# Moving the helper work of a fused attention and feed-forward kernel to other places of the step: constants, norm transposes and first weights

## The chip, the cores and the metric

The kernel runs on one core of a Trainium2 chip. The metric is the device time of one execution in microseconds (us); lower is better. A core has five engines that run their own instruction queues in order: PE (TensorE, matrix products), DVE (VectorE), ACT (ScalarE), POOL (GpSimd) and SP (SyncE, which here issues the DMAs). The PE writes into PSUM, which this kernel uses as six banks of 128 x 512 fp32 for products (tag "mm") and one double bank for attention scores (tag "st").

## The reference, cut to what matters

Two layers, each an attention over a context followed by a feed-forward, on 2048 tokens of width 512 (32 sequences of 64).

```python
x = x + L0_xattn(layernorm(x), ctx)      # 32 query heads, 8 key/value heads, rotary, softmax
x = x + L0_ffn(layernorm(x))             # gate and up weights 4-bit, group scales and zeros
x = x + L1_xattn(layernorm(x), ctx)      # like L0, with norms of q and k in place of the rotary
x = x + L1_ffn(layernorm(x))             # a small memory with a gate

# L0_ffn: w = sc[g] * (nibble(qw) - (nibble(qz[g]) + 1)), 512 x 2752 and 1376 x 512
w_gu = dequant(qweight_gu, qzeros_gu, scales_gu, g_idx_gu)
gate, up = (x @ w_gu)[..., :1376], (x @ w_gu)[..., 1376:]
out = (silu(gate) * up) @ dequant(qweight_down, qzeros_down, scales_down, g_idx_down)
```

The change touches the first attention (L0_xattn) and the way from it into L0_ffn.

## The kernel before, in words

**Tiling.** The 2048 tokens are four chunks of 512 (`NCH = 4`, index c). Attention goes over 8 key/value heads (index g, four query heads each) and, inside, over the four chunks: 32 **steps** (g, c), the loop in `Attention.run`. Large products are done as seven smaller ones instead of eight (a Strassen scheme, `PRODUCTS`, `quarters`), which needs sums of blocks first: `left_sums` and `right_sums`, four POOL instructions of 128 x 512 each.

**One step on the PE.** The loop is software-pipelined. In the pass for step i the PE does, in this order: the rest of the output products of step i-1 (`O`, 40 matmuls, `output_rest`), the key projection of step i+1 (`pk`), the query projection of step i+1 (`P`, 56 matmuls, `project_q`), the values' products of step i (`po`, 32), the value projection of step i+1 (`pv`, 32), the first output products of step i (`O`, 16, `output_first`), and the scores of step i+1 (`S`, 32). I count a step's length from one start of `pk` to the next.

**Beside it.** DVE does the softmax of step i while `output_rest` runs (`softmax`, a generator: mask on S L531, row maximum r2x and m1x, its spread mb L313, subtraction L581, sum r2s and m1s, reciprocal L586, spread ib L313), mixed with the additions of the output products to x (`join` L242). ACT does the exponential; POOL multiplies by the reciprocal sums (s L589). Then come the rotations (`rotate`): for k (rk) and for each of four quarters of q (rq), two ACT copies, a cosine product L424, a sine product L425 on DVE, and a sum on POOL L426 (kT, qT). The temporary tile of `rotate` (`tmp_tile`) has two buffers, shared with the constants below. POOL also makes the sums of the attention output (oT, `left_sums`, L166 to L169) in each step, in the steps with c = 0 the sums of the output weights (wo, `right_sums`, L174 to L177), and in the steps with c = 3 those of the next query weights (wq).

**Order.** Each engine's order is made ahead of time by a list scheduler: of the instructions that it takes to be ready, the one written first goes first; one that is not ready is passed over. `tc.issue_after(ins)` queues what a block emits on the engine of `ins` behind `ins`, without a wait, and leaves other engines alone.

**The pieces.** `ffn_constants` is a generator of 24 pieces that build the dequantisation tables of L0_ffn (scales split in three bf16 parts, zeros, one-hot group rows; tiles pidx, scales_gu, scales_down, qz, zi, g_idx_*, szoh). Through `late` one piece runs in each step of g = 1 to 6: one that prepares pidx (20 tiny instructions), seven of scales (three DMAs, then CAST, SCALAR_TENSOR_TENSOR, CAST, SCALAR_TENSOR_TENSOR, CAST), eight of zeros (shift, cast, shift, cast), eight of indices (one DMA, four instructions). All but the DMAs is DVE work. Before the change a piece is emitted just behind `output_rest`, and queued behind the last join (`self.added`).

**The way into the feed-forward.** When a chunk's last output is joined (g = 7, one step later), `joined` takes its norm statistics, and `after` scales it (xnb, DVE L272), transposes it on the PE (xtb, 16 matmuls L286), copies it (ACT L290, xnT) and makes its sums (POOL). In the pass for (7, c) this is done for chunk c-1. Before the change `after` is emitted ahead of `values` for c = 1 and 2, behind it for c = 3.

`ahead` has three hooks for the pass (7, 2), which bring in the first feed-forward weights wgu: `ffn_load` (8 DMAs), `ffn_dequant` for each quarter k of the rows (nibbles by a DVE shift L900, two matmuls pgz L917 that spread scales and zeros, two DVE instructions L895 and L896), and `ffn_sums` (POOL). Hook 0 stands behind `project_q`, hook 1 behind `values`, hook 2 ahead of `output_first`. In the last pass (7, 3), `tail` starts the feed-forward's first up product (`P<-xnT,wgu`).

Of the kernel before, what the change touches and what calls it, by code (L numbers as in the profile page):

```python
# [15 lines left out]
ALU = mybir.AluOpType  # L16
# [28 lines left out]
def tile_xattn_ffn_2_layers(ctx: ExitStack, tc: tile.TileContext, a: dict, out: bass.AP):  # L45
    nc = tc.nc
# [30 lines left out]
    def w_tile(name):  # L77
        return wp.tile([P, NBLK, 2, HC], F32, tag="w", name=name, bufs=2)
# [7 lines left out]
    def tmp_tile(name):  # L86
        return ap_.tile([P, 2, CH], F32, tag="tmp", name=name)
# [26 lines left out]
    sinT = const.tile([P, KH, 4, KB], F32, tag="sinT", name="sinT")  # L114
# [48 lines left out]
    def left_sums(t, width=HC, engine=nc.gpsimd):  # L163
        b = [t[:, k, :, 0:width] for k in range(NBLK)]
        tt = engine.tensor_tensor
        tt(b[4], b[2], b[3], ALU.add)  # L166
        tt(b[5], b[4], b[0], ALU.subtract)
        tt(b[2], b[0], b[2], ALU.subtract)
        return tt(b[6], b[1], b[5], ALU.subtract).ins  # L169
# [152 lines left out]
    class Attention:  # L322
# [94 lines left out]
        def rotate(self, name, src, dst, view, over):  # L417

            t = tmp_tile(name)
            h = HD // 2  # L420
            for lo, hi in ((0, h), (h, HD)):
                nc.scalar.copy(t[lo:hi, 1], src[HD - hi : HD - lo])  # L422
            x = t[:, 0] if src.space == bass.MemoryType.PSUM else src
            nc.vector.tensor_tensor(view(x), view(src), over(cosT), ALU.mult)  # L424
            nc.vector.tensor_tensor(view(t[:, 1]), view(t[:, 1]), over(sinT), ALU.mult)  # L425
            nc.gpsimd.tensor_tensor(dst(None), dst(x), dst(t[:, 1]), ALU.add)  # L426

        def project_q(self, g, c):
# [243 lines left out]
        def run(self, hooks, joined, after, between=lambda c: None, tail=lambda: None, late={},  # L672
                ahead=(lambda: None,) * 3):

            steps = [(g, c) for g in range(NKV) for c in range(NCH)]  # L680

            def ctx_of(i):
                return load_ctx(steps[i][1], f"{self.L}_{steps[i][0]}_{steps[i][1]}")

            before = None
            v = self.v
            ctxT = ctx_of(1)
            (kT, kpart), (qT, part) = self.state
            scales = self.norms(0, 0, kpart, part)
            st = self.scores(0, 0, kT, qT)  # L690
            for i, (g, c) in enumerate(steps):
                more = i + 1 < len(steps)
                if c == NCH - 1 and g + 1 < NKV:
                    self.load_kv(g + 1)
                for hook in hooks.get((g, c), ()):
                    hook()
                ctx_next = ctx_of(i + 2) if i + 2 < len(steps) else None
                if g == NKV - 1 and c > 1:
                    between(c - 2)
                pieces = self.softmax(g, c, st, scales)  # L700

                def middle():
                    if c == NCH - 1 and g + 1 < NKV:
                        with tc.issue_after(self.pooled):
                            left_sums(self.wq[g + 1])

                if before is not None:
                    probs = self.output_rest(*before, pieces, middle)
                    with tc.issue_after(self.added):
                        for hook in late.get((g, c), ()):  # L710
                            hook()
                else:
                    *_, probs = pieces
                if c == 0 and g > 0:
                    self.load_out(g)
                done = before is not None and before[0] == NKV - 1
                if done:
                    joined(before[1])
                if more:
                    kT, kpart = self.project_k(*steps[i + 1], ctxT)  # L720
                    if c == 0:
                        right_sums(self.wo[g])
                    qT, part = self.project_q(*steps[i + 1])
                    if c == NCH - 2 and g + 1 < NKV:
                        self.load_q(g + 1)
                    if i + 2 == len(steps):
                        ahead[0]()
                else:
                    tail()

                late_after = not more and self.L == 0
                if done and not late_after:
                    after(before[1])
                oT = self.values(g, c, v, probs)
                if done and late_after:
                    after(before[1])
                if i + 2 == len(steps):
                    ahead[1]()
                if more:
                    scales = []  # L740

                    def middle():
                        scales.append(self.norms(*steps[i + 1], kpart, part))

                    v = self.project_v(*steps[i + 1], ctxT, middle)
                    scales = scales[0]
                if self.L == 1 and more:
                    with tc.issue_after(self.pooled):
                        self.pooled = left_sums(oT)
                else:  # L750
                    self.pooled = left_sums(oT)
                if i + 2 == len(steps):
                    with tc.issue_after(self.pooled):
                        ahead[2]()
                before = self.output_first(g, c, oT)
                if more:
                    with tc.issue_after(last_matmul):
                        st = self.scores(*steps[i + 1], kT, qT)
                ctxT = ctx_next
            between(NCH - 2)  # L760
            self.output_rest(*before)
            joined(before[1])
# [97 lines left out]
    def ffn_load(i):  # L860
        f0, fw = groups[i]
        w = w_tile(f"wgu{i}")
        for k in range(KT):
            for j in range(2):
                nc.sync.dma_start(
                    w[:, 2 * j + k // 2, k % 2, 0:fw].bitcast(U32),
                    a["qweight_gu"][16 * k : 16 * k + 16, j * INTER + f0 : j * INTER + f0 + fw]
                    .unsqueeze(1)
                    .to_broadcast([16, 8, fw]),
                )  # L870
        wgu[i] = w
# [32 lines left out]
    def ffn_dequant(i, *parts):  # L904

        f0, fw = groups[i]
        sz, oh = ffn["sz"], ffn["oh"]
        w, d = wgu[i], wd[i] if i in wd else None
        for k in parts:
            if k < KT:  # L910
                wk = w[:, k // 2 : 4 : 2, k % 2, 0:fw]
                nibbles(wk, P)
                pp = [mm_tile(f"pgz{i}_{k}_{side}") for side in range(2)]
                for side, rows in enumerate(
                    (slice(R_GS, R_GS + 3 * NG), slice(R_GZ, R_GZ + NG))
                ):
                    nc.tensor.matmul(  # L917
                        pp[side][:, 0 : 2 * fw],
                        oh[rows, k * P : (k + 1) * P],
                        sz[rows, :].rearrange("p (j f) -> p j f", j=2)[:, :, f0 : f0 + fw],  # L920
                        start=True,
                        stop=True,
                    )
                pv = [x[:, 0 : 2 * fw].rearrange("p (j f) -> p j f", j=2) for x in pp]
                dequant(wk, pv[0], pv[1])
                continue
            if k - KT >= len(ffn_tiles(i)):
                continue
            t = k - KT
            f, w_ = ffn_tiles(i)[t]  # L930
            dt = d[0:w_, 2 * t : 2 * t + 2, 0, :]
            nibbles(dt, w_)
            pp = [mm_tile(f"pdz{i}_{t}_{side}") for side in range(2)]
            for side, rows in enumerate((slice(R_DS, R_DS + 3 * NGD), slice(R_DZ, R_DZ + NGD))):
                nc.tensor.matmul(
                    pp[side][0:w_, :], oh[rows, f : f + w_], sz[rows, 0:D], start=True, stop=True
                )
            dequant(dt, *(x[0:w_, :].rearrange("p (j w) -> p j w", j=2) for x in pp))

    def ffn_sums(i):  # L940
        left_sums(wgu[i], groups[i][1])
# [391 lines left out]
    def first_after(c):  # L1333
        norm_apply(c, "b")
        if c == last - 1:
# [7 lines left out]
        tail=ffn_first,  # L1343
        late={(g, c): [lambda: next(pieces, None)] for g in range(1, NKV - 1) for c in range(NCH)},
        ahead=(
            lambda: (ffn_load(0), ffn_dequant(0, 0, 1)),
            lambda: ffn_dequant(0, 2, 3),
            lambda: ffn_sums(0),
        ),
    )  # L1350

# [126 lines left out]
```

## Time and profile before

| | us |
|---|---|
| median of 3 runs | 2862.06 (2861.47 to 2863.86) |
| the profiled execution's own time | 2860.84 |
| its span, first to last instruction | 2859.1 |
| PE busy | 2804.8 (98%) |
| DVE busy | 1874.9 (66%) |
| POOL busy | 1318.9 (46%) |
| ACT busy | 834.0 (29%) |

Times in the timeline are us from the span's start. The first attention lies at about 15 to 1190 us, its feed-forward up to about 1600 us, the second attention after it. A busy share is an average; a PE that is 98% busy still has places where it waits, or where it counts as busy and runs slowly. The profile also gives the TensorE clock that was granted: over the whole span 0.995 of full speed.

### The profile page before, as it was taken

The numbers are of one execution on the slowest core, as the hardware profiler recorded it, in microseconds if no ns is written. First come the engines' busy times: TensorE is split into PE (matmuls) and PEld (weight loads), VectorE is DVE, ScalarE is ACT, GpSimd is POOL, SyncE is SP. The second block draws the span as 40 slices with busy tenths as digits, with TensorE's granted clock in tenths as the row PEclk, the third lists the DMA queues.
The fourth block names the chain that finished last, engine by engine and source line by source line (L and its number), as shares of the span: only waits on it lengthen the run. The fifth ranks groups of instructions, "written<-read, shape, count | busy, mean of one in ns | idle before, by whom it ended". The sixth has DMA issues, their size and how long they took to land. (4 is left out here: it accounts for less than half of the span.)

```text
span 2859.1 us, 41235 instructions
## 1 busy us (share of the span) xinstructions
PE 2804.8 (98%) x16742; PEld 2267.1 (79%) x16742; DVE 1874.9 (66%) x2814; ACT 834.0 (29%) x1410; POOL 1318.9 (46%) x1030
## 2 busy tenths in 40 slices
PE   7999999999999999999999999999999999999997
PEld 5878787888888887888888778888888888888775
DVE  7777777777777777665555655555555555555666
ACT  3333333333333333221111222222222222222333
POOL 5554545454545454544433444444444444444331
PEclk9999999999999999999999999999999999999999
DMA  4111111111111110100001101111111111111101
GB/s 159 38 52 46 53 46 53 44 53 45 53 47 52 50 55 15 45 23 22 16 13 33 52 30 59 45 52 45 52 45 52 45 52 45 52 45 52 30 1 59
DMA packets 103812, 130.77 MB, mean 46 GB/s; under 512 B 8725, under 2 KB 65165, under 8 KB 103623
## 3 DMA queue, kind: packets, MB, share of 16 engines
q1 hardware_dynamic: 103047, 127.09, 13.7%
q8 instruction: 133, 2.18, 0.3%
q10 hardware_dynamic: 576, 1.05, 0.1%
q14 instruction: 56, 0.46, 0.1%
HBM read 123.92 MB, written 4.19 MB: 45 GB/s over the span
## 5 line engine op out<-in xcount | busy, mean ns | idle before, releaser
L189 PE MATMUL O<-wo,oT 128*128 128x256 f32 x3584 | 802.4, 381 | 1.8 <-ACT oT L617 1.1
L189 PE MATMUL P<-xnT,wq 128*128 128x256 f32 x3584 | 788.2, 380 | 10.6 <-ACT h L214 10.4
L189 PEld LDWEIGHTS P<-xnT,wq 128*128 128x128 f32 x3584 | 681.1, 190 | 133.4 <-issue 31.5
L189 PEld LDWEIGHTS O<-wo,oT 128*128 128x128 f32 x3584 | 670.2, 190 | 115.5 <-issue 25.0
L242 DVE TENSOR_TENSOR x<-x,O 128x512 f32<-128x512 f32 (+1 forms) x448 | 368.4, 823 | 248.2 <-PE O L189 248.1
L589 POOL TENSOR_TENSOR s<-s,ib 128x512 f32<-128x512 f32 x128 | 169.4, 1344 | 529.9 <-DVE ib L313 514.0
L214 ACT COPY h<-P 128x512 f32<-128x512 f32 (+1 forms) x352 | 202.7, 576 | 561.2 <-PE P L189 559.4
L247 POOL TENSOR_TENSOR qr<-qs,nhalf 128x20 f32<-128x20 f32 x32 | 113.4, 3544 | 380.5 <-DVE qs L496 380.5
L426 POOL TENSOR_TENSOR qT<-h,rq 128x512 f32<-128x512 f32 x128 | 175.5, 1371 | 237.5 <-DVE rq L425 237.5
L583 ACT ACTIVATE s<-s 128x1024 f32<-128x1024 f32 x64 | 67.7, 1057 | 728.2 <-DVE s L581 728.2
L189 PE MATMUL P<-xnT,wgu 128*128 128x256 f32 (+1 forms) x1232 | 271.3, 380 | 0.2
L189 PEld LDWEIGHTS P<-xnT,wgu 128*128 128x128 f32 (+1 forms) x1232 | 229.8, 187 | 39.9 <-DVE x L242 4.1
L407 PE MATMUL pv<-wkv,ctxT 128*128 128x128 f32 x1984 | 248.2, 281 | 1.2 <-DVE h L439 1.2
L407 PEld LDWEIGHTS pv<-wkv,ctxT 128*128 128x128 f32 x1984 | 230.5, 193 | 23.1 <-issue 17.6
L375 PE MATMUL pk<-ctxT,wkv 128*128 128x512 f32 x496 | 223.2, 592 | 0.9 <-DVE h L439 0.9
L422 ACT COPY rq<-h 64x512 f32<-64x512 f32 x256 | 157.9, 617 | 123.6 <-DVE h L439 115.6
L424 DVE TENSOR_TENSOR h<-h,cosT 128x512 f32<-128x512 f32 x128 | 91.6, 716 | 123.0 <-ACT rq L422 122.8
L375 PEld LDWEIGHTS pk<-ctxT,wkv 128*128 128x128 f32 x496 | 94.1, 190 | 94.0 <-issue 89.6
L457 DVE TENSOR_TENSOR qT<-h,P 128x512 f32<-128x512 f32 x128 | 87.7, 686 | 100.8 <-PE P L189 94.7
L463 DVE TRANSPOSE_TENSOR_REDUCE part<-q 128x16 f32<-128x512 f32 x128 | 90.6, 708 | 87.8 <-ACT q L459 83.9
L960 DVE TENSOR_TENSOR h<-h,P 128x512 f32<-128x512 f32 (+1 forms) x96 | 61.2, 640 | 127.1 <-PE P L189 94.2
L967 POOL TENSOR_TENSOR hT<-h,h 128x512 f32<-128x512 f32 (+1 forms) x48 | 56.6, 1183 | 186.9 <-DVE h L960 186.9
(250 smaller groups left out, 3429.9 us busy)
## 6 DMA issues: line engine op xcount, KB each, us to landing
ctxT<-in_ctxT SPq DMA_DIRECT2D x62, 1024.0 KB
wq<-in_L_wq SPq DMA_DIRECT2D x32, 256.0 KB
wo<-in_L_wo SPq DMA_DIRECT2D x32, 256.0 KB
wq<-in_L_wqT SPq DMA_DIRECT2D x32, 256.0 KB
wo<-in_L_woT SPq DMA_DIRECT2D x32, 256.0 KB
wgu<-in_qweight_gu SPq DMA_DIRECT2D x40, 128.0 KB
out<-o SPq DMA_DIRECT2D x16, 256.0 KB
x<-in_x SPq DMA_DIRECT2D x12, 256.0 KB
```

Of the source, the lines that this page charges most:

```text
L189: ins = nc.tensor.matmul(pv[0:w, m, :], left[:, l, k, m * P : m * P + w], right[:, r, k, :], start=(first and m == 0 and k == 0), stop=(k ...
L214: last_copy = nc.scalar.copy(t[size], ps[size]).ins
L242: return nc.vector.tensor_tensor(dst, dst, src, ALU.add).ins
L247: return nc.gpsimd.tensor_tensor(dst, src, nhalf[:, : src.shape[-1]], ALU.pow).ins
L375: nc.tensor.matmul(ps, wkv[:, k, 0, :], ctxT[:, k, :], start=(k == 0), stop=(k == KT - 1))
L407: nc.tensor.matmul(ps[:, t * HD : (t + 1) * HD], ctxT[:, k, t * P : (t + 1) * P], wkv[:, k, 1, :], start=(k == 0), stop=(k == KT - 1),)
L422: nc.scalar.copy(t[lo:hi, 1], src[HD - hi : HD - lo])
L424: nc.vector.tensor_tensor(view(x), view(src), over(cosT), ALU.mult)
L426: nc.gpsimd.tensor_tensor(dst(None), dst(x), dst(t[:, 1]), ALU.add)
L457: nc.vector.tensor_tensor(q, xv, yv, ALU.add)
L463: nc.vector.tensor_reduce(part[:, i, f], q2.rearrange("p (g q) -> p g q", q=KB), AX.X, ALU.add, apply_transpose=True,)
L589: nc.gpsimd.tensor_tensor(sv[:, f], sv[:, f], ib[:, f * W : (f + 1) * W].unsqueeze(1).to_broadcast([P, KH, W]), ALU.mult,)
```

## The change

Three things are moved; no arithmetic is changed.

1. A piece of `ffn_constants` is emitted behind `project_v` of the pass in place of behind `output_rest`, and its DVE work is queued behind `self.turned`, the last sine product of the next queries' rotation.
2. In L0, for the passes (7, 1) and (7, 2), `after` (norm scaling, transposes, copies, sums) is emitted behind the sums of oT, thus behind `values` and `project_v`, ahead of `output_first`; its POOL work is queued behind those sums. The pass (7, 3) and L1 keep their order.
3. The hooks of `ahead`: hook 0 only issues the load; hook 1 (now behind `after`, ahead of `output_first`) dequantises quarters 0 and 1; hook 2 (now behind `output_first`) quarters 2 and 3, and the sums.

```diff
@@ rotate
-            nc.vector.tensor_tensor(view(t[:, 1]), view(t[:, 1]), over(sinT), ALU.mult)
+            self.turned = nc.vector.tensor_tensor(
+                view(t[:, 1]), view(t[:, 1]), over(sinT), ALU.mult
+            ).ins
@@ run
                     probs = self.output_rest(*before, pieces, middle)
-                    with tc.issue_after(self.added):
-                        for hook in late.get((g, c), ()):
-                            hook()
...
-                late_after = not more and self.L == 0
-                if done and not late_after:
+                if done and self.L == 1:
                     after(before[1])
                 oT = self.values(g, c, v, probs)
-                if done and late_after:
+
+                if done and self.L == 0 and not more:
                     after(before[1])
-                if i + 2 == len(steps):
-                    ahead[1]()
...
                     v = self.project_v(*steps[i + 1], ctxT, middle)
                     scales = scales[0]
+                    for hook in late.get((g, c), ()):
+                        with tc.issue_after(self.turned):
+                            hook()
...
                     self.pooled = left_sums(oT)
+                if done and self.L == 0 and more:
+                    with tc.issue_after(self.pooled):
+                        after(before[1])
+                if i + 2 == len(steps):
+                    ahead[1]()
+                before = self.output_first(g, c, oT)
                 if i + 2 == len(steps):
                     with tc.issue_after(self.pooled):
                         ahead[2]()
-                before = self.output_first(g, c, oT)
@@ att0.run
         ahead=(
-            lambda: (ffn_load(0), ffn_dequant(0, 0, 1)),
-            lambda: ffn_dequant(0, 2, 3),
-            lambda: ffn_sums(0),
+            lambda: ffn_load(0),
+            lambda: ffn_dequant(0, 0, 1),
+            lambda: (ffn_dequant(0, 2, 3), ffn_sums(0)),
         ),
```

## The prediction

> **What bounds it.** The page's first row says that the PE is the bound; the question is where it loses time. For that I listed the PE's timeline and took the distance between starts of `pk`, one step each.
>
> ```profile
> PE 2804.8 (98%) x16742; PEld 2267.1 (79%) x16742; DVE 1874.9 (66%) x2814; ACT 834.0 (29%) x1410; POOL 1318.9 (46%) x1030
> ...
> 300.48 3.60 PE L375 MATMUL pk<-ctxT,wkv 128*128 128x512 f32 x8
> 335.86 3.60 PE L375 MATMUL pk<-ctxT,wkv 128*128 128x512 f32 x8
> 372.55 3.60 PE L375 MATMUL pk<-ctxT,wkv 128*128 128x512 f32 x8
> ...
> 1082.93 3.60 PE L375 MATMUL pk<-ctxT,wkv 128*128 128x512 f32 x8
> 1098.83 1.91 PE L286 MATMUL xtb<-ident,xnb 128*128 128x128 f32 x16
> 1103.06 2.48 PE L609 MATMUL po<-s,v 32*128 32x256 f32 x26 [1.26 <-ACT xnT L290]
> 1123.29 3.60 PE L375 MATMUL pk<-ctxT,wkv 128*128 128x512 f32 x8
> 1139.30 0.60 PE L917 MATMUL pgz<-szoh 12*128 12x512 bf16 x4
> 1143.43 1.97 PE L286 MATMUL xtb<-ident,xnb 128*128 128x128 f32 x8 [1.96 <-ACT xnT L290]
> 1152.83 5.86 PE L407 MATMUL pv<-wkv,ctxT 128*128 128x128 f32 x32
> 1172.67 12.25 PE L189 MATMUL P<-xnT,wgu 128*128 128x256 f32 x56
> ```
>
> The reader is to see this: a step takes 35.38 us (335.86 - 300.48). Nearly all steps of L0 from 120 to 1083 do; those longer are the ones with c = 0 and a piece: from 191.79 by 2.55, from 335.86 by 1.31, from 478.80 by 1.95, from 622.26, 763.79 and 905.45 by 0.02, 0.14, 0.59, and one other by 0.11: 6.7 together. The step from 1082.93 takes 40.36, and from the end of `P` at 1139.30 to the feed-forward's first product at 1172.67 pass 33.37. Then the windows around 1140, each 3.41 long (columns: PE, PEld, DVE, ACT, POOL busy, granted clock, DMA share, GB/s):
>
> ```profile
> 1102.47:1105.88 3.41, 2.82 (x29) 2.21 (x30) 2.33 (x2) 2.73 (x6) 2.59 (x2) 1.00 0.00 0
> 1140.02:1143.43 3.41, 1.25 (x9) 0.84 (x9) 2.64 (x6) 3.11 (x6) 1.42 (x2) 1.00 0.50 146
> 1143.43:1146.84 3.41, 3.41 (x14) 2.82 (x14) 3.41 (x4) 1.61 (x3) 2.72 (x3) 0.50 0.58 169
> 1150.26:1153.67 3.41, 3.41 (x18) 1.86 (x11) 2.32 (x4) 2.05 (x4) 2.37 (x3) 0.50 0.00 0
> 1153.67:1157.08 3.41, 3.41 (x18) 3.41 (x18) 1.15 (x2) 0.00 (x0) 3.33 (x3) 0.50 0.01 2
> ```
>
> After a window with the PE busy for 1.25 us, four windows (1143.43 to 1157.08, 13.65 us) run at half clock: `pv` took 5.86 there against 3.84 in other steps. The PE counts as busy in them, so no list of waits shows this loss.
>
> **Norms and first weights (parts 2 and 3).** The cause is PSUM banks. In front of `po`, the four pgz of hook 0 and the four transpose tiles of `after` want eight of the six banks; the pgz are freed only by DVE (L895, from 1146.89), which waits for the rotation and the load, and the transposes wait for ACT, whose queue holds the rotation's copies. Behind `pv` the rotation is done (its last sine product ends about 6.2 us after `P`; `po` and `pv` take 5.6), ACT has emptied the four banks of `po` during `pv`, and one bank goes every 0.5 us to an xnT copy.
>
> *Step from 1082.93*: 40.36 - 35.38 - 1.84 for the transposes themselves (1098.83 to 1100.67) = 3.1 saved. *From 1139.30*: start to start in other rows, po 1.94, pv 3.67, xtb 1.84, O 3.55, S 1.86, O 8.74, pgz for eight about 1.2 (twice the 0.6 row): 22.8, so 10.6 saved, some 6.8 of it half clock (13.65 x 0.5). Together 13.7.
>
> [...] The rows show half clock with a busy share of 1.25/3.41, and none with 2.82/3.41. I take the rows: 10.6.
>
> What is late next: DVE. From the end of the rotation (about 1145) it must do four nibble shifts (0.5 each, up to 1.5 beside POOL), eight dequant instructions of 0.68, nine joins and the softmax of (7, 3): 23 us, so ib comes at about 1168 and s, 2.5 later, at 1171; `po` of (7, 3) is then due at 1139.3 + 22.8 + 12.2 = 1174.3. The wgu sums on POOL, behind those of oT and xnT (four of 1.27 each), end near 1164 against a product that starts at 1162 but uses unsummed blocks first. The eight wgu DMAs stay where they were on SP (they need the old weights' buffer), so nothing on that queue moves. I put 1.3 for stalls here (0 to 3: the covers are 2 to 3 us).
>
> **Pieces (part 1).** Taking the piece from in front of rk saves the 6.7. What it meets in the new place is in DVE's and POOL's timelines:
>
> ```profile
> 374.36 0.35 DVE L806 CAST scales_gu<-scales_gu 12x512 bf16<-12x512 f32 x1
> 376.00 1.37 DVE L806 CAST scales_gu<-scales_gu 12x512 bf16<-12x512 f32 x1
> ...
> 360.80 1.27 POOL L166 TENSOR_TENSOR oT<-oT 128x512 f32<-128x512 f32 x1
> 364.61 2.25 POOL L169 TENSOR_TENSOR oT<-oT 128x512 f32<-128x512 f32 x1
> ...
> 363.95 1.79 DVE L531 COPY_PREDICATED S<-minv,neg 128x1024 f32<-128x1024 uint8 x1 [1.21 <-PE S L508]
> ```
>
> One CAST takes 0.35 alone and 1.37 beside POOL's s: it waits for POOL's instruction to end. In the new place POOL makes the oT sums. The last rotation ends at 359.43 and the mask on S is due at 363.95; two joins take 1.4 of this, so 3.1 are free. A scales piece alone (0.35 + 0.70 + 0.35 + 0.70 + 0.41 = 2.5) would fit, cost 0. Beside POOL each instruction waits for one sum: its load's packets end at 360.70, the CAST gets in at 362.1, then sum and piece take turns (1.27 + 0.35, 1.27 + 0.70, ...) to about 368, then mask and last CAST, so r2x starts at about 369.5 in place of 365.77: the softmax is late by d = 3.7. In the same way indices 2.9, zeros 2.5 (first four) and 0.9 (last four, 0.19 and 0.31 an instruction). [...]
>
> What d costs. In a plain step ib ends 2.9 after the start of pk, and rk starts at 4.95 (1052.50 - 1047.55); at 6.87 (379.42 - 372.55) the step still lasts 35.38, at 7.87 and 10.64 it lost 1.95 and 2.55. So the limit is near 8.1, and d up to 5.2 is free: nothing in c = 1; in c = 2 and 3, where POOL also sums wq, scales reach 5.5: 0.6 in all. With c = 0, POOL does s, the wo sums and then kT, which frees the buffer of a q rotation: its ACT copy stands at 13.85 without a piece; steps lost 0.02 at 14.11, 0.59 at 14.67, 1.31 at 15.40. So loss is about d - 1.3. The pieces that lie ahead of a c = 0 softmax are those of c = 3: scales twice 2.4, zeros 1.2 and 0, indices twice 1.6: 9.2. Part 1 is thus -6.7 + 9.2 + 0.6 = +3.1. Its ends: -6.7 (no wait) and +14 (every wait in full, one POOL instruction each).
>
> **Sum.** -13.7 + 1.3 + 3.1 = -9.3 on the profiled execution's 2860.84 gives 2851.5; the median of the runs lies 1.2 higher: 2862.06 - 9.3 = **2853**. Later half-clock windows, 3.41 long, fall otherwise once all is earlier: plus or minus 2.
>
> **Rivals.** *Pieces cost nothing* (chance 0.20): the scheduler passes them over until POOL is quiet, or kT goes ahead of wo. -13.7 + 1.0 - 6.7 = -19.4, 2843. For it: 3.1 us of free DVE; against: the sums fill that time.
> *The bank shortage moves along* (0.20): pgz hold four banks behind xtb until DVE has dequantised, and `O` starves; half clock stays. Only the first step's 3.1 and 1.5 of gaps are saved, pieces +3.1: -1.5, 2860.5. For it: six banks, and DVE is later still; against: nibbles can be done during `pv` and xtb.
> *Pieces delay every softmax* (0.13), slower: the place is DVE behind the rotation in all 24 steps. It loses (d - 5.2) in 18 and (d - 1.3) in 6 steps, and saves 19.4 elsewhere, so it decides from d = 4.7 to 5. At the upper bound, 5.7, it costs 9 + 26 = 35: +16, 2878. For it: five instructions with a wait each; against: only the seven scales pieces have that many.
> *The forecast* has 0.47, its own range 2848 to 2857. What a measurement can tell from no change is about 0.2%, 5.7 us. Faster by more: nearly all of 0.47 and 0.20, 0.66; same: the bank rival and the edge of the forecast, 0.22; slower 0.12. The range 2841 to 2862 leaves out the last rival and the tails.
>
> **What would show it.** Right: xtb behind pv in the PE timeline, steps at 1083 near 37.2, a granted clock of 1.00 from 1130 to 1170, steps with c = 1 at 35.38, those with c = 0 from g = 2 longer by 0 to 2.5, with L806 to L848 beside oT. Wrong: 0.50 still in that stretch, or plain steps above 35.38 throughout.

## The result: slower; the norms gained what was foretold, the pieces cost seven times what was foretold

The changed kernel takes **2871.68 us** (median of 8 runs, 2869.74 to 2874.70), the kernel before 2862.84 (8 runs on the same chip, 2861.19 to 2867.67). The ratio is 1.0028, with a 95% interval of 1.0019 to 1.0038. The prediction was 2853, with a range up to 2862.

Busy time by engine in the changed kernel, its costliest group of instructions, and the same group before the change:

```profile
PE 2804.3 (98%) x16742; PEld 2260.7 (79%) x16742; DVE 1900.7 (66%) x2814; ACT 832.7 (29%) x1410; POOL 1325.4 (46%) x1030
...
L189 PE MATMUL O<-wo,oT 128*128 128x256 f32 x3584 | 809.2, 382 | 21.6 <-DVE x L242 20.3
...
L189 PE MATMUL O<-wo,oT 128*128 128x256 f32 x3584 | 802.4, 381 | 1.8 <-ACT oT L617 1.1
```

The first row tells nothing: PE has the same busy time as before (2804.3 against 2804.8). The other two tell nearly all. The numbers behind the bars are the busy time, the mean in ns, and the idle time of the PE just ahead of the group with what ended most of it. Before, the output products `O` had 1.8 us of idle time ahead of them; now they have 21.6, and 20.3 of these end with a join of `O` to x (L242) on DVE.

The place is in the PE's timeline. Columns: start, duration, engine, line, operation; in brackets the idle time ahead and what ended it.

```profile
229.09 3.60 PE L375 MATMUL pk<-ctxT,wkv 128*128 128x512 f32 x8
...
255.73 1.99 PE L189 MATMUL O<-wo,oT 128*128 128x256 f32 x8
259.24 7.14 PE L189 MATMUL O<-wo,oT 128*128 128x256 f32 x32 [1.52 <-DVE x L242]
266.22 3.60 PE L375 MATMUL pk<-ctxT,wkv 128*128 128x512 f32 x8
...
297.33 5.42 PE L189 MATMUL O<-wo,oT 128*128 128x256 f32 x24 [2.48 <-DVE x L242]
...
305.18 3.60 PE L375 MATMUL pk<-ctxT,wkv 128*128 128x512 f32 x8
```

From `pk` to `pk` this step takes 37.13 us and the next 38.96, where a plain step took 35.38. Each has a hole behind the first eight of the forty matmuls of `output_rest`, that is, behind product 4 and ahead of product 6; the second step has another, of 0.60, ahead of product 7. The 27 steps from 121.63 to 1104.84 take 27.9 us more than 27 times 35.38; before it was 6.6 (from 121.04 to 1082.93). So the pieces cost **21.3** in place of the 3.1 predicted. The 27.9 are 18.5 in ten plain steps (c = 1, 2, 3) and 9.4 in steps with c = 0.

The way into the feed-forward is as predicted. The PE's timeline there:

```profile
1126.45 1.91 PE L286 MATMUL xtb<-ident,xnb 128*128 128x128 f32 x16
...
1158.76 2.01 PE L611 MATMUL po<-s,v 32*128 32x256 f32 x32
...
1164.38 1.91 PE L286 MATMUL xtb<-ident,xnb 128*128 128x128 f32 x16
...
1182.62 12.25 PE L189 MATMUL P<-xnT,wgu 128*128 128x256 f32 x56
```

The transposes xtb stand behind `pv`, and the 32 matmuls of `po` run through in 2.01; in the rows shown of before, `po` was cut by waits for the copies of xnT (1.26 in the step from 1082.93). From the end of `P`, where `po` starts, to the feed-forward's first product pass 23.86, where 33.37 lay between the same points before. The half clock is gone too: all windows from 1139.94 to 1177.45 have a granted clock of 1.00. The one with the least work for the PE ahead of `po` (columns: busy time of PE, PEld, DVE, ACT, POOL, then the granted clock, DMA share, GB/s):

```profile
1153.58:1156.99 3.41, 2.88 (x14) 2.22 (x13) 2.34 (x4) 1.97 (x4) 1.07 (x1) 1.00 0.01 2
```

The account of the two profiled executions, whose spans are 2859.1 and 2868.6: +0.6 at the start (84.55 against 83.96 at the third `pk`), +21.3 for the pieces, -2.85 in the step of 40.36, -9.1 from there to the next layer's first `pk` (481.52 to 472.41), -0.4 behind it. That is +9.5, the difference of the spans.

### The profile page after: what moved, and what is told of

Same layout as the page of the kernel before. It is cut to its first block, busy times and chain, and to the rows that moved or that the text cites. A ratio compares the mean times of both kernels' runs of the same rounds, so it can differ in the third digit from the quotient of the medians.

```text
span 2868.6 us, 41226 instructions
## 1 busy us (share of the span) xinstructions
PE 2804.3 (98%) x16742; PEld 2260.7 (79%) x16742; DVE 1900.7 (66%) x2814; ACT 832.7 (29%) x1410; POOL 1325.4 (46%) x1030
## 5 line engine op out<-in xcount | busy, mean ns | idle before, releaser
L189 PE MATMUL O<-wo,oT 128*128 128x256 f32 x3584 | 809.2, 382 | 21.6 <-DVE x L242 20.3
L242 DVE TENSOR_TENSOR x<-x,O 128x512 f32<-128x512 f32 (+1 forms) x448 | 368.4, 823 | 176.6 <-PE O L189 173.4
```

The lines of the kernel that those rows point to most:

```text
L189: ins = nc.tensor.matmul(pv[0:w, m, :], left[:, l, k, m * P : m * P + w], right[:, r, k, :], start=(first and m == 0 and k == 0), stop=(k ...
L242: return nc.vector.tensor_tensor(dst, dst, src, ALU.add).ins
```

## Why the output products wait

`output_first` makes product 1 in a bank x, joins it to the output (L242), then makes product 2. A step later `output_rest` makes product 4, and then adds product 6 **into the same bank x**: `x = self.out_product(g, c, oT, 1)` there, `self.out_product(g, c, oT, 6, x)` here. Product 6 may not start before the join of product 1 has read the bank (it starts at 259.24, 0.14 behind that join's end). Product 7 is added into x once more, so it waits for the join of product 6. Three joins of one bank thus stand in DVE's queue, mixed with the softmax.

DVE's timeline of the changed kernel beside the hole at 257.7:

```profile
252.19 1.10 DVE L810 CAST scales_gu<-scales_gu 12x512 bf16<-12x512 f32 x1 [1.82 <-DMA scales_gu<-in_scales_gu]
253.32 1.64 DVE L811 SCALAR_TENSOR_TENSOR scales_gu<-scales_gu,pidx 12x512 f32<-12x512 bf16 x1
...
258.09 0.41 DVE L812 CAST szoh<-scales_gu 12x512 bf16<-12x512 f32 x1
258.43 1.46 DVE L242 TENSOR_TENSOR x<-x,O 128x512 f32<-128x512 f32 x2
259.81 1.23 DVE L533 COPY_PREDICATED S<-minv,neg 128x1024 f32<-128x1024 uint8 x1
261.06 1.25 DVE L570 TRANSPOSE_TENSOR_REDUCE r2x<-S 128x32 f32<-128x1024 f32 x1
```

and of the kernel before, in its step from 229.72, which had no piece there, with the PE's row of the forty matmuls below it:

```profile
252.88 0.69 DVE L242 TENSOR_TENSOR x<-x,O 128x512 f32<-128x512 f32 x1 [1.87 <-PE O L189]
254.61 0.69 DVE L242 TENSOR_TENSOR x<-x,O 128x512 f32<-128x512 f32 x1 [1.04 <-PE O L189]
256.50 2.06 DVE L531 COPY_PREDICATED S<-minv,neg 128x1024 f32<-128x1024 uint8 x1 [1.20 <-PE S L508]
258.60 1.25 DVE L568 TRANSPOSE_TENSOR_REDUCE r2x<-S 128x32 f32<-128x1024 f32 x1
...
256.37 8.90 PE L189 MATMUL O<-wo,oT 128*128 128x256 f32 x40
```

Before, DVE waited 1.87 us for product 1 and joined it at once; the join ended at 253.57. Product 6 followed product 4 without a hole at about 258.1 (256.37, the start of product 4, and a fifth of the 8.73 to the next `pk` at 265.10). So the join was **4.55 us early**. Now the five instructions of the piece stand ahead of it, each but the last longer than 1 us. Counted from `pk`, the join starts at 29.34 in place of 23.16: 6.2 late against 4.55 of cover, a hole of 1.5 to 1.6. The softmax (r2x) is late by 3.1 only, since DVE had idle time between the joins and the mask. Its delay was the one that I had priced.

That delay does not reach the PE. The softmax's last spread ib and the rotation of k behind it, in the changed kernel's next step:

```profile
269.77 0.71 DVE L313 STREAM_TRANSPOSE ib<-m1s 128x512 f32<-128x512 f32 x1
...
271.17 0.69 DVE L424 TENSOR_TENSOR rk<-pk,cosT 128x512 f32<-128x512 f32 x1 [0.69 <-ACT rk L422]
```

The rotation rk starts 4.95 after `pk` (271.17 - 266.22), as in a plain step of before without a piece, and waits for ACT's copy, not for ib. It does so in every step from 157.00 to 1069.32 but one (5.22). Nor does the PE wait for ACT ahead of any `P` in them.

## The experiments

Two theories were open at first. **A**: the joins behind the piece hold the PE, through bank x. **B**: the late softmax holds it, through the later rotation and kT. All ratios are to the kernel before on the same chip.

**1. The parts alone.** `e1_norms_weights` has the change with the pieces in their old place; `e2_pieces` has only the pieces moved.

```diff
 # e1: the changed kernel, and behind output_rest again
+                    with tc.issue_after(self.added):
+                        for hook in late.get((g, c), ()):
+                            hook()
...
 # both behind project_v: e1 takes it away, e2 adds it to the kernel before
                     for hook in late.get((g, c), ()):
                         with tc.issue_after(self.turned):
                             hook()
```

> Only the norms' transposes and the first weights are moved; the pieces stay behind output_rest. Theory (the loss lies in the pieces alone, about 21 us of the changed kernel's steps from 192 to 1083): the way into the feed-forward keeps its gain, steps from pk of (7,2) on like in the changed kernel (37.5 and 9 us less to the next layer), so 2862.8 - 12 = 2851, steps of g = 1 to 6 as before the change. Rival (the two parts need each other, the loss partly in the norms): slower than 2857.

> Only the pieces are moved behind the rotation; norms and weights as before. Theory: steps with a scales piece take 37 to 40 us as in the changed kernel, and half clock before the feed-forward returns: 2862.8 + 21 = 2884. Rival (loss and gain are not separate): under 2875.

Measured: 2851.11 us for e1 (ratio 0.9957, interval 0.9945 to 0.9970) and 2885.83 for e2 (1.0077, 1.0064 to 1.0091). So norms and weights bring 11.7, and the pieces cost 23.0. The two sum to +11.3; the whole change has +8.8, and as the intervals reach about 3 to 4 us to both sides, nothing speaks for the parts acting on each other. In e2 the step with the norms of (7, 1) is as before (40.40), and the earlier steps lose 30.8 together, near the changed kernel's 27.9; two of them, from 264.43 and 778.92, lose 0.8 and 1.2 more than there. The loss lies in the pieces' new place.

**2. Without the sums on POOL.** `e9_no_sums` is the changed kernel, in which layer 0 for g = 1 to 6 leaves out the block sums of oT: ACT copies of other blocks stand in for them, so its output differs.

```diff
+                elif self.L == 0 and 0 < g < NKV - 1:
+                    for to, of in ((4, 2), (5, 0), (6, 1)):
+                        nc.scalar.copy(oT[:, to], oT[:, of])
```

> The changed kernel with the POOL sums of the attention output left out in g = 1 to 6 of L0 (ACT copies stand in for three of the blocks), so the output products there are of other numbers. Theory (the piece is long because each of its instructions waits for a POOL sum): a scales piece takes 2.5 us and less than 3.5 in place of 6.3, the first join is done in time, and all plain steps of g = 1 to 6 last 35.4. Rival (the place ahead of the first join is what costs, contention or not): the steps with scales stay above 36.5.

Measured in a single run: 2845.45 us. DVE's timeline in the step that had the hole at 257.7:

```profile
249.12 0.41 DVE L813 CAST scales_gu<-scales_gu 12x512 bf16<-12x512 f32 x1 [1.81 <-DMA scales_gu<-in_scales_gu]
249.56 0.74 DVE L814 SCALAR_TENSOR_TENSOR scales_gu<-scales_gu,pidx 12x512 f32<-12x512 bf16 x1
...
251.56 0.41 DVE L815 CAST szoh<-scales_gu 12x512 bf16<-12x512 f32 x1
251.90 1.46 DVE L242 TENSOR_TENSOR x<-x,O 128x512 f32<-128x512 f32 x2
```

The same five instructions take 2.85 us (249.12 to 251.97) in place of 6.31. Every plain step is 35.38 but three, and so are those with c = 0. The three (37.15, 36.09, 36.57) have the query weights' sums, which stayed on POOL; there the piece is drawn out again (1.64 and 1.38 for the instructions that took 0.74 and 0.41, in the step from 261.39), and holes of 1.53, 0.48 and 0.95 ahead of product 6 remain. The edit frees POOL and adds copies on ACT as well, but the piece's length is read from its own rows. In the changed kernel's step the first four instructions of the piece each end 0.28 or 0.54 behind the POOL sum beside them (sums L166 to L169, which end at 253.01, 254.42, 256.10 and 257.51). So the sums on POOL make the piece long, as the prediction had it, and the piece alone would have fitted.

**3. The piece behind both joins.** `e3_behind_join` queues it behind the second join of `output_first`.

```diff
-                    for hook in late.get((g, c), ()):
-                        with tc.issue_after(self.turned):
-                            hook()
...
                 before = self.output_first(g, c, oT)
+                for hook in late.get((g, c), ()):
+                    with tc.issue_after(self.added):
+                        hook()
```

> The changed kernel, with the pieces queued behind the second join of output_first in place of ahead of the first: same work, two joins of 0.69 us earlier on DVE. Theory A (product 6 adds into the bank of product 1 and waits for that bank's join, which stood behind the whole piece): the gaps inside O go, plain steps with scales return to about 35.4, what stays is the softmax being late, at most 2.5 in the six c = 0 steps: 2851 to 2858. Theory B (the softmax chain being late, through its effects on the rotation and on free banks, makes the loss): the piece still stands ahead of the mask on S, so the steps stay at 37 and more: 2868 to 2874.

Measured: 2877.9 us (1.0055, 1.0041 to 1.0069). The total missed what theory A expected by some 20 and lies outside B's interval too. Three steps went as A said: those from 228.42, 302.19 and 374.28 (scales, c = 1 or 3) are back at 35.38, without a hole. Others became longer. In the step from 263.80 (c = 2, 38.39 long) the instructions of the piece now stand in the middle of the softmax on DVE:

```profile
294.74 1.74 DVE L811 SCALAR_TENSOR_TENSOR scales_gu<-scales_gu,pidx 12x512 f32<-12x512 bf16 x1
...
297.58 0.37 DVE L812 CAST szoh<-scales_gu 12x512 bf16<-12x512 f32 x1
...
299.04 1.26 DVE L242 TENSOR_TENSOR x<-x,O 128x512 f32<-128x512 f32 x2
```

and on the PE:

```profile
290.44 7.17 PE L189 MATMUL O<-wo,oT 128*128 128x256 f32 x32
300.36 1.99 PE L189 MATMUL O<-wo,oT 128*128 128x256 f32 x8 [2.75 <-DVE x L242]
```

Thirty-two matmuls run through (products 4, 6, 5 and 3); the hole has moved ahead of product 7, which waits for the join of product 6. What the PE waits for is again a join of bank x. Against B speaks that in the steps from 302.19 and 374.28 ib ends 5.1 after `pk` (4.3 in the changed kernel's step from 266.22), and yet they take 35.38.

**4. Only product 1's join ahead.** This is the cleaner test: the order on DVE is that of the changed kernel, but the first join stands ahead of the piece, and the second among its first instructions. The softmax stays behind the piece.

```diff
             self.out_add(c, 0, 0, x)
+            self.first_join = self.added
...
                 before = self.output_first(g, c, oT)
+                for hook in late.get((g, c), ()):
+                    with tc.issue_after(self.first_join):
+                        hook()
```

> The changed kernel with one edit in layer 0: the join of output product 1 goes ahead of the piece on DVE, and product 2's join stays behind the piece's first instructions, so the mask on S and the softmax are about as late as in the changed kernel. Theory A (the plain steps lose because product 6 adds into the bank of product 1, whose join is queued behind the piece): the gap inside O in front of product 6 (1.52 in the step from 229.09, 2.48 in that from 266.22) is gone, steps with c = 1 and a scales piece are back at 35.38, those with c = 2 at 36 or less; the ten plain steps lose 18.5 together now, so up to 18.5 comes back: 2853 to 2860 us. Rival B (the later softmax itself is the price, through rk and kT): r2x starts as late, the steps stay at 37.1 and above, and the time is 2868 us or more.

Measured: 2861.02 us (10 runs, 2858.88 to 2863.82; ratio 0.9992, 0.9983 to 1.0001), 10.7 below the changed kernel's 2871.68 (the kernels before of the two series, 2862.67 and 2862.84, agree to 0.2). DVE's timeline in the step from 228.63:

```profile
251.79 0.69 DVE L242 TENSOR_TENSOR x<-x,O 128x512 f32<-128x512 f32 x1 [1.87 <-PE O L189]
252.40 0.45 DVE L811 CAST scales_gu<-scales_gu 12x512 bf16<-12x512 f32 x1
...
259.23 1.25 DVE L570 TRANSPOSE_TENSOR_REDUCE r2x<-S 128x32 f32<-128x1024 f32 x1
```

and the PE's there and in the following step:

```profile
255.28 9.22 PE L189 MATMUL O<-wo,oT 128*128 128x256 f32 x40
264.34 3.60 PE L375 MATMUL pk<-ctxT,wkv 128*128 128x512 f32 x8
...
290.98 7.17 PE L189 MATMUL O<-wo,oT 128*128 128x256 f32 x32
299.62 1.99 PE L189 MATMUL O<-wo,oT 128*128 128x256 f32 x8 [1.47 <-DVE x L242]
301.46 3.60 PE L375 MATMUL pk<-ctxT,wkv 128*128 128x512 f32 x8
```

The reader is to see that all forty matmuls run through in the first step: the hole of 1.52 is gone and the step takes 35.71. Yet r2x starts 30.60 after `pk`, 1.7 later than before, and ib ends 4.31 after the next `pk`, as late as in the changed kernel (4.26). So a softmax that is late by that much costs nearly nothing. In the second step (c = 2, with sums of the query weights beside the piece) the hole ahead of product 6 is gone too, but one of 1.47 ahead of product 7 is left: 37.12 in place of the 36 or less expected. The plain steps lose 9.9 in place of 18.5. The steps with c = 0 still lose 8.5, and in those from 337.16 and from 482.10 the wait (1.04 and 1.50) is also that of product 7 for the join of product 6. Theory A holds, but with two waits in place of one; the total came out 1 us above the expected interval because of the second. B has nothing left in plain steps with c = 1 and 3: it asked for 37.1 and more, and they take 36.25 at most. One thing differs from what was expected of r2x: it comes 1.4 earlier after `pk` than in the changed kernel, as the first join runs in time in which the piece had waited for its load. This run alone thus leaves open what 3.1 at r2x would cost; that rk starts at 4.95 in the changed kernel itself closes it.

**5. Another order of the products.** `e8_five_first` puts product 5 ahead of product 6, to give the join of product 1 one product more of time.

```diff
             self.out_add(c, 1, 0, z)
+            five = self.out_product(g, c, oT, 5)
             self.out_product(g, c, oT, 6, x)
             self.out_add(c, 0, 1, x)
...
-            self.out_add(c, None, 1, self.out_product(g, c, oT, 5), 1)
+            self.out_add(c, None, 1, five, 1)
```

> The changed kernel with output product 5 (a bank of its own, 1.75 us) ahead of product 6, which adds into the bank of product 1. Theory (product 6 waits for the join of product 1): it is due 1.75 us later, so the plain steps with scales go from 37.14 to about 35.4 and the steps of c = 2 passes from 38.0 to 39.0 lose that much too; about 15 us less in L0, 2857, unless product 5 now waits for a free bank. Rival (the PE waits for any free bank, or for the late softmax): product 5 takes a new bank and the steps stay at 37.1 or grow.

Measured: 2964.96 us (1.0352, 1.0335 to 1.0369), over 100 above what was expected. The edit stands in both layers, and the plain steps of layer 1, which have no pieces at all, went from 35.83 to 37.25 and, in places, up to 40.15. The PE's timeline in layer 0:

```profile
262.35 7.21 PE L189 MATMUL O<-wo,oT 128*128 128x256 f32 x32
272.26 3.05 PE L189 MATMUL O<-wo,oT 128*128 128x256 f32 x8 [2.69 <-DVE x L242]
```

and DVE's:

```profile
269.64 0.71 DVE L313 STREAM_TRANSPOSE mb<-m1x 128x512 f32<-128x512 f32 x1
270.38 1.23 DVE L583 TENSOR_TENSOR s<-S,mb 128x1024 f32<-128x1024 f32 x1
271.53 1.93 DVE L242 TENSOR_TENSOR x<-x,O 128x512 f32<-128x512 f32 x2
```

The hole ahead of product 6 is gone, as meant. But product 6 now comes 1.8 later while product 7 stays where it was, so only product 3 lies between them, and the join of 6 falls behind mb and s of the softmax. The granted clock is lower as well: 0.989 over the span, against 0.996 in the changed kernel. In layer 1 the same wait is 1.15 and 2.53 in the steps from 1727.32 and 1764.57. The run doesn't tell A from B; it shows that the order 4, 6, 5, 3, 7 is tight at both ends.

**6. Norms and weights apart.** `e6_transposes_only` moves only `after`, `e12_weights_only` only the hooks of `ahead`.

```diff
 # e6
+                if done and self.L == 0 and more:
+                    with tc.issue_after(self.pooled):
+                        after(before[1])
...
 # e12
-            lambda: (ffn_load(0), ffn_dequant(0, 0, 1)),
-            lambda: ffn_dequant(0, 2, 3),
-            lambda: ffn_sums(0),
+            lambda: ffn_load(0),
+            lambda: ffn_dequant(0, 0, 1),
+            lambda: (ffn_dequant(0, 2, 3), ffn_sums(0)),
```

> Only the norms (scaling, transposes, copies, sums) are moved; hooks of the weights and pieces as before. Theory (pgz and transposes together ask for more than the banks, and pgz hold theirs until DVE is through the rotation): pgz ahead of the values' products still hold four of six banks, the values wait, the half clock stays; from pk of (7,2) to the next layer 478 to 482 against 481.5 before and 472.4 changed; the step of (7,1) is 37.5. Rival (the transposes alone make the wait): 472 to 474.

> Only the hooks of the first weights are moved; norms and pieces as before. Theory: no pgz ahead of the values, the transposes alone cost here what they cost in the step of (7,1), about 3 us, and no half clock: 475 to 476 from pk of (7,2) to the next layer; the step of (7,1) stays at 40.4. Rival (both parts are needed): 479 to 482 with half clock.

Measured in one run each: 2858.46 and 2855.55 us. With e6 the earlier step falls to 37.53, but the stretch to the next layer stays at 480.25 (before 481.52). With e12 that stretch falls to 474.47; the earlier step is 41.96 in place of the 40.4 expected, as a window in it (1104.01 to 1107.42) ran at half clock. Both totals contain one more such window near 205, outside the parts that were moved, so the stretches say more than the totals. Of the pair, the hooks hold most of the gain at the end of the attention, and both are needed for all of it. The PE's timeline of e6 shows what the pgz ahead of `po` still do:

```profile
1138.35 0.60 PE L921 MATMUL pgz<-szoh 12*128 12x512 bf16 x4
1139.37 2.50 PE L611 MATMUL po<-s,v 32*128 32x256 f32 x16 [0.41 <-DVE h L441]
1142.48 2.77 PE L611 MATMUL po<-s,v 32*128 32x256 f32 x16 [0.62 <-ACT oT L619]
1146.67 6.06 PE L407 MATMUL pv<-wkv,ctxT 128*128 128x128 f32 x32 [1.42 <-DVE wgu L899]
```

`pv` waits for DVE to empty a bank (wgu, L899) and then runs at half clock, 6.06 in place of 3.84, though no transposes are in the way any more.

**7. The pieces in the old place, but never with c = 0.** `e5_skip_c0` and `e11_spread` have the norms and weights of the change, and other steps for the pieces.

```diff
-        late={(g, c): [lambda: next(pieces, None)] for g in range(1, NKV - 1) for c in range(NCH)},
+        late={
+            (g, c): [lambda: next(pieces, None)] * {(4, 1): 3, (4, 2): 2}.get((g, c), 1)
+            for g in range(NKV - 1)
+            for c in range(1, NCH)
+        },
```

This is e11; e5 starts at (0, 2) and has triples and doubles at (4, 2), (4, 3) and (6, 3).

> Norms and weights moved as in the change; the pieces in their old place behind output_rest, but none in a step with c = 0 (they start at (0,2), and steps (4,2), (4,3) and (6,3) take 3, 2 and 2). Theory (in the old place a piece is free unless POOL makes the wo sums): the 6.7 us of the c = 0 steps go too, 2862.8 - 12 - 6 = 2845, up to 1.5 more for the doubled ones. Rival (the pieces' waits only move to other steps): 2851 as with the old places.

> The norms and first weights of the change, the pieces in their old place but in no step with c = 0: they begin two steps earlier, at (0, 1), run over c = 1 to 3, and double up only with zeros and indices at (4, 1) and (4, 2). Theory: in the old place a piece costs nothing where c is not 0, so the whole of layer 0 from 121 on runs at 35.38 but for what doubled pieces cost (below 0.5 a step), and the time is some 1 to 2 us below the version with pieces in triples (2846.66): 2845 us. Rival: pieces ahead of g = 1 meet the start of the kernel, where the steps are not yet regular, and cost 1 to 3: 2847 to 2849.

Measured: 2846.66 us for e5 (0.9942, 0.9928 to 0.9956) and **2843.93** for e11 (0.9933, 0.9920 to 0.9945). Both beat the two kernels of this case. In e11 all 27 steps from 122.21 take 35.38 but one of 35.43. The pieces in (0, 1) cost 0.8 in the step from 84.30 (37.91 in place of 37.08), less than its rival's 1 to 3. In e5 the doubled index piece at (6, 3) had cost 1.8.

## Why the prediction was wrong, step by step

- **Norms and first weights: right.** Foretold -13.7 + 1.3 = -12.4. In the two traces it is -2.85 (foretold -3.1) and -9.1 over the stretch to the next layer; between the end of `P` and the feed-forward's first product it is -9.5 (foretold -10.6 + 1.3 = -9.3). e1 has -11.7 by medians.
- **The clock: right.** Half clock went with the bank shortage, as the row of 1.25 busy in 3.41 had said: 13.65 us at half clock before (1143.43 to 1157.08), none from 1139.94 to 1177.45 in the changed kernel.
- **The old loss of 6.7: right.** e11 runs through those steps at 35.38.
- **The piece beside POOL: right in kind.** That each instruction of a piece waits for one sum was an estimate from one row, the CAST of 1.37, which ended at 377.37, 0.28 behind the first of POOL's two s (377.09). e9 agrees: 0.41 and 0.74 an instruction without the sums, against 1.10 to 1.64 beside them in the changed kernel. What makes the instruction wait was not shown. As to d, r2x was late by 3.1 against the 3.7 foretold for scales.
- **"In a plain step ... d up to 5.2 is free": the step that failed.** The limit was taken from one consumer of DVE's work, the chain from softmax to rk. I wrote "two joins take 1.4 of this" and counted the joins as filling, without asking who waits for them. The diff queues the piece ahead of them, and product 6 needs the first one within 4.55. The term for plain steps was put at 0.6 and came out at 18.5. The rows that would have given it stand in the stretch of before in which I looked for free time on DVE: the join of product 1 ends at 361.02, and product 6 was due 4.5 later (363.81 and a fifth of 8.74).
- **The steps with c = 0: right size, wrong reason.** Foretold 9.2 through kT and the buffers of the rotation. Of the measured 9.4, waits for joins make 4.5: 1.08 and 2.49 in the steps from 192.38 and 342.33, the second with a half-clock window behind it (some 1.7 more), and 0.3 in each of three others (495.06, 779.94, 925.64). The rest is spread over small losses, such as waits of `pv` of 0.17, and is not explained one by one. None of these steps has a wait of `P` for ACT, which the kernel before had in three of them. So the loss by kT that I priced did not come, and others took its place; that the sum agrees is luck.
- **The rival on the slower side** was near in sign and in place, DVE behind the rotation. But it let only a d above about 4.7 decide, with the softmax as the carrier. It needed a d of 5.7 for its +16; the +8.8 came with r2x late by only 3.1 in a step with c = 1, because the join there was late by 6.2 against a cover of 4.55.

What stays open: why some steps with a piece lose about 0.3 without a visible wait (35.70 and 35.69 in the changed kernel's steps from 567.04 and 638.12). In both the time goes into output products that run drawn out (9.22 for the forty in place of 8.90, 3.84 for the sixteen in place of 3.62); the records give no cause.

## What to carry to other kernels

When work is put into an engine's queue, list everything that stands behind it there, find for each who reads it next and how early it was, and take the smallest of these covers as the limit; the instruction that looks like filling may have the shortest. A PSUM bank that is added into again in the next step has such a reader (here with a cover of 4.55 us), and a reordering that gives one of its joins more time can take it from the next (in `e8_five_first` a hole of 2.69 ahead of product 7). If a helper costs nothing in most places and something in few, spread it over the good places before moving it to a new one.

## What the hardware showed that was not expected

In the traces of the kernels before and after, between 60 and 2760 us, the half clock came in stretches of 3.41 us or, once, four times that (13.65), and the length of a hole alone did not tell whether one followed. In the kernel before, the stretches from 1143.43 and 1648.60 lie 505.17 us apart, which is 148 windows of 3.413. The windows below lie on such a grid, each kernel's on its own. Two holes of the changed kernel are equally long, 2.48 (294.86 to 297.33) and 2.49 (371.45 to 373.94). The windows around both:

```profile
292.92:296.34 3.42, 1.94 (x11) 1.38 (x8) 3.35 (x3) 0.00 (x0) 3.39 (x3) 1.00 0.55 204
296.34:299.75 3.41, 2.42 (x11) 2.19 (x12) 3.31 (x4) 0.00 (x0) 3.36 (x3) 1.00 0.01 4
...
371.43:374.84 3.41, 0.92 (x5) 0.85 (x5) 3.27 (x5) 0.00 (x0) 0.78 (x1) 1.00 0.00 0
374.84:378.25 3.41, 3.41 (x9) 2.68 (x9) 3.34 (x5) 0.00 (x0) 0.00 (x0) 0.50 0.03 5
```

The first hole is split between two windows, busy for 1.94 and 2.42, and costs no clock. The second falls within one, busy for 0.92, and the next window runs at half. The same old hole of 2.28 ahead of `P` shows it again. In the kernel before (204.03 to 206.31) two windows share it, busy for 2.67 and 1.87, and the step takes 37.93. In e6 (203.09 to 205.37) one window holds all of it, and the step takes 39.62:

```profile
202.46:205.87 3.41, 1.13 (x5) 0.67 (x5) 2.04 (x4) 1.82 (x3) 1.27 (x1) 1.00 0.00 0
205.87:209.28 3.41, 3.41 (x9) 2.67 (x9) 2.04 (x4) 1.79 (x3) 1.27 (x1) 0.50 0.00 0
```

Between 60 and 2760 us of the traces before and after, four windows at full clock were followed by half clock. The PE was busy in them for 1.25 (1140.02) and 0.66 (1645.19) before, and for 0.92 (371.43) and 0.39 (1654.84) in the changed kernel. In all others it was busy for 1.87 or more, and none was followed by half clock. But in e6 one of 2.79 was (1141.07 to 1144.48), where `po` was cut by waits. How busy the PE was in one window thus does not tell all. Nor is it known why four windows in a row ran at half clock at the norms' place in the kernel before (1143.43 to 1157.08), while the hole of 2.49 inside `O` cost one in the changed kernel (374.84 to 378.25); this was not tried.
